# Layer 0 of a two-layer attention network: the evictions, the first head pair's fills and the output projection in another order

## The chip, the cores and the metric

The kernel runs on one core of one Trainium2 chip. A core has a matrix engine (TensorE, PE in the profile, with its weight loads as PEld), three engines for elementwise work (VectorE = DVE, ScalarE = ACT, GpSimd = POOL) and SyncE (SP), which here only issues DMA transfers. Each engine runs its own instructions in the order in which the program has them; semaphores tie the engines together. TensorE writes its results into PSUM, from where VectorE or ScalarE must take them before the space can be used again. ScalarE issues DMA transfers too, in line with its other work.

The metric is the device time of one execution in microseconds (us), and less is better. The kernel before the change took 2998.03 us, the median of three runs (2995.43 to 3001.4).

## What is computed

Eight images of 384 channels and 32 x 32 pixels (1024 tokens) go through two layers. The change is in layer 0, which the reference gives as follows (cut):

```python
def _L0_conv_ref(x, qkv_w, qkv_b, proj_w, proj_b, ...):          # x is the group norm of the image
    tokens = x.reshape(b, c, n).transpose(0, 2, 1)
    qkv = (tokens @ qkv_w + qkv_b).reshape(b, n, 3, NUM_HEADS, HEAD_DIM)   # 8 heads of 48
    q, k, v = ...
    attn = jnp.einsum('bhnd,bhmd->bhnm', q * scale, k)
    attn = jax.nn.softmax(attn + _relative_bias(h, w, ...)[None], axis=-1)
    out = jnp.einsum('bhnm,bhmd->bhnd', attn, v)
    out = out.transpose(0, 2, 1, 3).reshape(b, n, c) @ proj_w + proj_b
    return out.transpose(0, 2, 1).reshape(b, c, h, w)
x = x + _L0_conv_ref(_gn(x), ...)
```

Layer 1 (attention with normalized q and k, and a feed-forward block with quantized activations) follows. The change does not touch it.

## The kernel before

Layer 0 goes image by image (`for b in range(B)`). For each image its q, k and v are computed, then the scores, their exponentials and the weighted values in batches, and last the output projection. The heads are taken as four pairs. A tile of q or k has 128 rows, 64 for each head of a pair: 48 rows (`D0`) are the head's own, and 16 more (`FR`) belong to the fourth pair, whose 48 rows are computed 16 at a time in the spare rows of the three other pairs. So there are six blocks of q and k products, `BLOCKS0` = (pair 0, k), (pair 0, q), (1, k), (1, q), (2, k), (2, q); this text counts them as blocks 0 to 5.

For images 1 to 7 the products run in a form in which each float is cut into a coarse part and a rest. `Ahead.products` (line 664) makes three groups of six matmuls for a block, two into a PSUM tile `pg` and one into a PSUM tile `pm`. `Ahead.take` (line 670) empties them: ScalarE takes `pm` into an SBUF tile `t` (L687), VectorE adds `pg` (L691). `halves` (line 696) then cuts `t` again: ScalarE rounds it into the upper half (L700; `k`, `q` or `th` in the profile) and VectorE subtracts that to have the lower half (L701). Both halves of a block of pair 1 or 2 are stored to HBM (`self.there`, shown as `halves`), the upper half on ScalarE's DMA queue and the lower half on SyncE's (L705: 512 KB each; L707: the 16 spare rows of each head, 64 KB each). Pair 0 is used at once and isn't stored, except for its spare rows.

The scores of a batch use three operand tiles for k and two for q. For k they are the upper half, the lower half, and one mixed tile. In each of them the spare 16 rows, or all 64, must be filled with rows of the other half. For pairs 1 to 3 that happens when they are loaded back (`load_k`, `load_q`). For pair 0 the `move` function (line 714) does it with SBUF to SBUF transfers, `PIECES`: for q six transfers (four of 128 KB into the mixed tile, two of 64 KB into the upper half), for k eight (four of 128 KB into the mixed tile, two of 64 KB into each half). In the profile they are the L716 lines. The pieces for the mixed tile go out in `halves`; the others are handed back and run after the next block's `take`.

Four PSUM tiles of two banks each (`mm2`) are all there is for TensorE's results, taken in turn: two for a block of q and k products, two for a quarter of v (`project_v`, L772, emptied on VectorE at L780 and L784), one for each score product, one for the weighted values and one for each third of the output projection.

The attention of images 1 to 7 is a list of 16 batches per image (`Batches.run`, line 905). A batch makes four score products (L916), VectorE adds the relative bias to each (L923), ScalarE takes exponentials (L927), and TensorE weighs the values (L889) one batch later. Between the score products of a batch and the end of the one before, `between` does other work for units 2n and 2n + 1 of batch n. Unit 3, which is in batch 1, makes the output projection of the image before (`project_out`, L993 and L1009): 36 matmuls over `oT`, with the residual `res` added on VectorE and the result stored by SyncE (L1012).

`oT` holds the weighted values. `divide` normalizes them by a trip through HBM: SyncE stores the sums (L951, L953), GpSimd inverts them (L954), SyncE spreads the inverse (L958, L966), GpSimd multiplies (`multiply`, L970). For the fourth pair SyncE then moves 16 rows each to the places of the three other pairs (L980, six transfers of 64 KB). `later` is a list of work that comes due after so many steps; `take` and `project_v` count as steps.

The crossing from one image to the next (lines 1153 to 1204) emits: blocks 0 and 1 of the next image with their `take`; then block 2, a quarter of v, `halves`, the three other quarters of v; then blocks 3 to 5, each with its `take` and `halves`; then the loads of `res`; then batch 0 of the next image. In `take`, the halves of a block are emitted right behind its eviction, and so stand ahead of the next block's eviction in ScalarE's and VectorE's order. Only block 5's halves are held until `between` of batch 0.

All transfers of ScalarE and SyncE use eight completion semaphores in turn, in the order in which the scheduler has them, and each waits until the transfer that had its semaphore before, eight transfers earlier, has landed. The list of the built program shows these waits for both kernels.

Of the kernel before, what the change touches and what calls it, by code (L numbers as in the profile page):

```python
# [19 lines left out]
F32 = mybir.dt.float32  # L20
F32R = mybir.dt.float32r
AF = mybir.ActivationFunctionType
ALU = mybir.AluOpType
# [16 lines left out]
NP0 = H0 // 2  # L40
NF0 = NP0 - 1
FR = D0 // NF0
# [21 lines left out]
CUT = 4096.0  # L64
# [38 lines left out]
BLOCKS0 = [(0, 1), (0, 0), (1, 1), (1, 0), (2, 1), (2, 0)]  # L103
# [97 lines left out]
class _Weights:  # L201
# [74 lines left out]
def _layer0(tc, ins, x1, sums, shared, weights, beside):  # L276
# [4 lines left out]
    nc = tc.nc  # L281
    x = ins["x"]
# [3 lines left out]
    with ExitStack() as ctx:  # L286
        const = ctx.enter_context(tc.tile_pool(name="a_const", bufs=1))
        qkp = ctx.enter_context(tc.tile_pool(name="a_qk", bufs=2 * NP0 + 1))
# [9 lines left out]
        def flat2(t):  # L298
            return t.rearrange("p h q -> p (h q)")

        later = _Later()
# [4 lines left out]
        SP = S0 - D0  # L306
# [20 lines left out]
        for g in range(P // QT):  # L327
            at = g * QN
            n = min(QN, NREL - at)
# [104 lines left out]
        oT = kept.tile([P, NP0, N], F32, tag="oT", name="oT")  # L434
# [162 lines left out]
        BB = len(BLOCKS0) // 2  # L597
# [35 lines left out]
        class Ahead:  # L633
# [34 lines left out]
                cuts.products(n, i, self.ps[n, i // 2], self.parts[i])  # L668

            def take(self, n):  # L670
                pair, s = BLOCKS0[n]
                name = f"{self.b}_{pair}_{s}"
                here = pair == 0
                t = rest = qkp.tile([P, N], F32, tag="qk", name="t" + name)
                if here and s == 1:
                    self.k[pair] = self.k_tiles(pair)
                elif here:
                    self.q[0] = [
                        qkp.tile([P, N], F32R, tag="qk", name=f"q{i}" + name) for i in range(2)
                    ]  # L680
                    for h in range(NH):
                        self.q[0, h] = [q[:, ts(h, HALF)] for q in self.q[0]]
                else:
                    high = qkp.tile([P, N], F32R, tag="qk", name="th" + name)
                ps = self.ps.pop((n, 0)), self.ps.pop((n, 1))
                by = D0**-0.5 if s == 0 else 1.0
                nc.scalar.activation(  # L687
                    t, flat2(ps[1]), AF.Identity, scale=-by / CUT,
                    bias=bq[:, pair : pair + 1] if s == 0 else bqk[:, s, pair : pair + 1],
                )  # L690
                nc.vector.scalar_tensor_tensor(  # L691
                    t, flat2(ps[0]), by * (1.0 + 1.0 / CUT), t, ALU.mult, ALU.add
                )
                later.step()

                def halves():
                    up, down = (self.q[0] if s == 0 else self.k[0][:2]) if here else (high, rest)
                    if here and s == 0:
                        down = t
                    nc.scalar.copy(up, t)  # L700
                    nc.vector.tensor_sub(down, t, up.bitcast(F32))  # L701
                    for x, (queue, part) in enumerate(((nc.scalar, up), (nc.sync, down))):
                        part = part.bitcast(F32)
                        if not here:
                            queue.dma_start(self.there[s, pair, x], part)  # L705
                        for j in range(2):
                            queue.dma_start(  # L707
                                self.there[s, NF0, x, j * S0 + pair * FR : j * S0 + (pair + 1) * FR],
                                part[j * S0 + D0 : (j + 1) * S0],
                            )  # L710
                    if not here:
                        return []

                    def move(to, row, n, x, at):
                        for j in range(2):
                            (nc.sync if x or row == D0 else nc.scalar).dma_start(  # L716
                                to[j * S0 + row : j * S0 + row + n].bitcast(F32),
                                (up, down)[x][j * S0 + at : j * S0 + at + n].bitcast(F32),
                            )

                    tiles = self.q[0] if s == 0 else self.k[0]
                    for piece in PIECES[s][-1]:
                        move(tiles[-1], *piece)
                    return [
                        lambda to=to, of=of: move(to, *of[1]) for to, of in zip(tiles[:-1], PIECES[s])
                    ]

                return halves

            def k_tiles(self, pair):  # L730
                return [
# [210 lines left out]
        def divide(b, pair):  # L942


            o = oT[:, pair]
            sd = dram.tile([2, N], F32, tag="sd", name=f"sd{b}_{pair}")
            rd = dram.tile([2, N], F32, tag="rd", name=f"rd{b}_{pair}")
            mine = sums[:, b, pair]
            inv = kept.tile([P, 2 * N // P], F32, tag="inv", name=f"inv{b}_{pair}", bufs=2)
            for j in range(2):  # L950
                nc.sync.dma_start(sd[j : j + 1], oT[j * S0 : j * S0 + 1, pair])  # L951
            with nc.allow_non_contiguous_dma(reason="sums"):
                nc.sync.dma_start(mine, sd.rearrange("j (p c) -> (j p) c", c=2 * N // P))  # L953
                nc.gpsimd.tensor_tensor(inv, mine, over.to_broadcast([P, 2 * N // P]), ALU.pow)  # L954

            def keep_inverse():
                with nc.allow_non_contiguous_dma(reason="sums"):
                    nc.sync.dma_start(rd.rearrange("j (p c) -> (j p) c", c=2 * N // P), inv)  # L958

            later.after(2, keep_inverse)  # L960
            rb = []

            def spread():
                rb.append(kept.tile([P, N], F32, tag="rb", name=f"rb{b}_{pair}"))
                for j in range(2):
                    nc.sync.dma_start(rb[0][ts(j, S0)], rd[j].partition_broadcast(S0))  # L966
                later.after(2, multiply)

            def multiply():
                nc.gpsimd.tensor_mul(o, o, rb[0])  # L970
                if b == B - 1:
                    if pair < NF0:
                        for j in range(2):
                            nc.gpsimd.memset(oT[j * S0 : j * S0 + SP, pair], 0.0)
                elif pair == NF0:

                    for c in range(NF0):
                        for j in range(2):
                            row = j * S0 + SP + c * FR
                            nc.sync.dma_start(  # L980
                                oT[j * S0 : j * S0 + SP, c], oT[row : row + FR, pair]
                            )

            later.after(2 if pair == NF0 else 3, spread)

# [52 lines left out]
        parts = [(h, c) for h in range(H0) for c in range(4)]  # L1038
# [16 lines left out]
        for i in range(len(parts) // 2):  # L1055
            later.after(i + (13 if i < 9 else 12), lambda: grow_turns(1))
            at = 1 + i % NF0 if i < 12 else 2 + i % 2
            later.after(i + 10, lambda at=at: grow_loads(1, at))
        qk = project_qk(0, first)
# [17 lines left out]
        for b in range(B):  # L1077

            def beside_unit(i):
                nonlocal xn, ahead, cuts, res  # L1080
                if i == (16 if b == 0 else 1) and b + 1 < B:
                    xn = load(b + 1)
                    for at, stage in zip(
# [1 line left out]
                        group_norm(b + 1, xn),  # L1085
                    ):
                        later.after(at, stage)
                if i == 3 and b > 0:
                    project_out(b - 1, res, range(NF0))
                if b == B - 1:  # L1090
                    for at, work in beside:
# [10 lines left out]
                if b in (1, 2, 3) and i == 12:  # L1102
                    t = shared.weights(f"cw{b}")
# [5 lines left out]
                if b + 1 < B:  # L1109
                    if i == masks[0]:  # L1110
                        ahead = Ahead(b + 1, xn)
# [59 lines left out]
            for k in range(KC):  # L1171
                ahead.mixed(k)

            waits = []

            def take(n):
                nonlocal held_halves
                halves = ahead.take(n)
                if n < BB:
                    cuts.load(n + BB)  # L1180
                if n == BB - 1:
                    ahead.project_v(0)
                while waits:
                    waits.pop(0)()
                if n < len(BLOCKS0) - 1:
                    waits.extend(halves())
                else:
                    held_halves = halves

            for n in range(2):  # L1190
                for i in range(2):
                    ahead.products(cuts, n, i)
            for n in range(2):
                ahead.products(cuts, n, 2)
                take(n)
            for n in range(2, len(BLOCKS0)):
                for i in (2, 0, 1):
                    ahead.products(cuts, n, i)
                take(n)
                if n == BB - 1:  # L1200
                    for m2 in range(1, MT // 2):
                        ahead.project_v(m2)
            place = shared.weights(f"res{b}")
            res = residuals(b, lambda name, place=place: place[:, ts(int(name[-1]), N)])

# [1351 lines left out]
```

## Time and profile before

| | us |
|---|---|
| median of three runs | 2998.03 |
| the profiled execution's own time | 3001.04 |
| its span, first to last instruction | 2999.2 |
| TensorE busy in it | 2900.5 (97%) |
| VectorE busy | 2020.1 (67%) |
| ScalarE busy | 1555.8 (52%) |
| layer 0, eight images with its preparation, ends at about | 1430 |

The page's slices show TensorE at nine tenths or more of nearly every slice in the second half, and at eight tenths in some of the first, where layer 0 runs. These dips come back once for each image. DMA is used most in the same half (150 to 220 GB/s in most slices). A busy share is an average, so it doesn't show where the lost time is; for this one asks for the busy time of stretches of the timeline.

### The profile page before, as it was taken

To read this page: it belongs to the slowest core of one execution; us is meant where nothing else is said; L and a number is where in the kernel's file an instruction comes from. 1 tells how busy PE (TensorE), PEld (TensorE's weight loads), DVE (VectorE), ACT (ScalarE), POOL (GpSimd) and SP (SyncE) were. 2 spreads that over 40 slices of the span, in tenths; PEclk is the share of its full clock that TensorE was granted. 3 is DMA by queue.
4 is the path that set the end of the run, shared out by engine and by line. 5 is a ranking of instruction groups with operands and counts; after the bars stand their busy time and mean duration, and the time that the engine had idled before them with its cause. 6 is when DMAs were issued, how large, how long until landed. Compare 5 with 4: busy or idle time off the path is not lost.

```text
span 2999.2 us, 43573 instructions
## 1 busy us (share of the span) xinstructions
PE 2900.5 (97%) x16850; PEld 1656.4 (55%) x16850; DVE 2020.1 (67%) x2041; ACT 1555.8 (52%) x1888; POOL 492.4 (16%) x318
## 2 busy tenths in 40 slices
PE   8999989899998989989999999999999999999999
PEld 3464554645455464644545656746756746755553
DVE  3976858677675867756474685685785775775746
ACT  2654626454462645445372474574564564564644
POOL 3120202112020211103201301302302302302020
PEclk9999999999999999999999999999999999999999
DMA  7656475655647465473420121211312202112111
GB/s 192 188 170 185 134 216 132 183 158 149 183 119 210 113 181 148 139 206 80 136 76 24 35 78 50 64 53 50 87 31 59 92 21 78 69 39 82 39 45 38
DMA packets 177752, 324.78 MB, mean 108 GB/s; under 512 B 75745, under 2 KB 94673, under 8 KB 176257
## 3 DMA queue, kind: packets, MB, share of 16 engines
q1 hardware_dynamic: 166880, 298.04, 34.5%
q10 hardware_dynamic: 10656, 23.85, 2.9%
q8 instruction: 137, 2.24, 0.3%
q14 instruction: 79, 0.64, 0.1%
HBM read 227.50 MB, written 80.65 MB: 103 GB/s over the span
## 4 chain that ended last, share of the span: by engine, by line
PE 83%; DVE 7%; ACT 4%; DMA 3%; issue 2%; ACTq 1%; SPq 0%; POOL 0%; DVEq 0%
PE o L889 13%; PE s L1909 11%; PE o L1958 11%; PE s L916 9%; PE y2p L2203 6%; PE pg L171 5%; PE y1p L2152 5%; PE pp L993 4%; PE pv L1846 4%; PE pp L2055 3%; PE pm L171 2%; PE s L820 2%; PE pq L1698 1%; DVE t L691 1%; DVE e L923 1%
## 5 line engine op out<-in xcount | busy, mean ns | idle before, releaser
L927 ACT ACTIVATE e<-e 128x1024 f32<-128x1024 f32 x448 | 473.7, 1058 | 271.0 <-DVE e L923 246.2
L923 DVE TENSOR_TENSOR e<-s,grow 128x1024 f32<-128x1024 f32 x448 | 516.9, 1217 | 72.5 <-PE s L916 66.2
L1920 ACT ACTIVATE e<-s,kc 128x512 f32<-128x512 f32 x768 | 464.0, 694 | 172.1 <-PE s L1909 161.3
L889 PE MATMUL o<-e,v 128*64 128x512 f32 x1792 | 416.9, 609 | 24.4 <-DVE e L923 24.4
L1909 PE MATMUL s<-qk,qk 64*64 64x512 f32 x3072 | 418.7, 592 | 1.2 <-DVE oT L1968 1.1
L1958 PE MATMUL o<-e,v 64*64 64x512 f32 x3072 | 414.3, 590 | 0.0
L916 PE MATMUL s<-q,k 64*128 64x512 f32 x2688 | 358.1, 411 | 28.1 <-ACT t L687 24.4
L916 PEld LDWEIGHTS s<-q,k 64*128 64x128 f32 x2688 | 253.5, 192 | 170.3 <-DVE e L923 38.8
L889 PEld LDWEIGHTS o<-e,v 128*64 128x64 f32 x1792 | 123.8, 139 | 262.7 <-issue 242.4
L1935 DVE TENSOR_TENSOR t<-t,e 128x1024 f32<-128x1024 f32 x192 | 231.0, 1221 | 46.0 <-ACT e L1920 45.9
L1909 PEld LDWEIGHTS s<-qk,qk 64*64 64x64 f32 x3072 | 153.9, 132 | 191.2 <-issue 108.9
L1958 PEld LDWEIGHTS o<-e,v 64*64 64x64 f32 x3072 | 159.3, 133 | 169.4 <-issue 142.3
L954 POOL TENSOR_TENSOR inv<-sums,over 128x16 f32<-128x16 f32 x32 | 93.2, 2913 | 845.2 <-DMA sums<-sd 653.4
L2139 DVE TENSOR_REDUCE parts<-y 128x1 f32<-128x1024 f32 x75 | 89.7, 1217 | 103.3 <-ACT y L2136 102.8
L1932 DVE TENSOR_TENSOR t<-e,e 128x1024 f32<-128x1024 f32 x96 | 114.2, 1224 | 59.5 <-ACT e L1920 59.5
L1815 POOL TENSOR_TENSOR hc<-hc,rsqrt 128x32 f32<-128x32 f32 x24 | 141.3, 5888 | 2.0
L1846 PE MATMUL pv<-wv,bx 128*128 128x384 f32 x384 | 128.3, 491 | 0.0
L2055 PE MATMUL pp<-oT,L_attn_proj_wT 128*128 128x512 f32 x288 | 126.3, 595 | 2.1 <-DVE oT L2021 2.1
L993 PE MATMUL pp<-oT,wp 128*128 128x512 f32 x288 | 125.7, 595 | 0.0
L1846 PEld LDWEIGHTS pv<-wv,bx 128*128 128x128 f32 x384 | 119.4, 314 | 9.8 <-ACT e L1920 4.1
L970 POOL TENSOR_TENSOR oT<-oT,rb 128x1024 f32<-128x1024 f32 x32 | 77.5, 2422 | 264.8 <-DMA rb<-rd 131.1
L2152 PE MATMUL y1p<-lun,w 128*128 128x512 f32 x360 | 113.5, 396 | 2.6 <-DVE lun L2102 2.6
(239 smaller groups left out, 4023.9 us busy)
## 6 DMA issues: line engine op xcount, KB each, us to landing
rb<-rd SPq DMA_DIRECT2D x110, 256.0 KB
wc<-cut SPq DMA_DIRECT2D x42, 576.0 KB
k<-halves SPq DMA_DIRECT2D x84, 192.0 KB
wc<-there SPq DMA_DIRECT2D x25, 576.0 KB
halves<-th ACTq DMA_DIRECT2D x28, 512.0 KB
halves<-t SPq DMA_DIRECT2D x28, 512.0 KB
xn<-in_x_dram SPq DMA_DIRECT2D x24, 512.0 KB
res<-in_x_dram SPq DMA_DIRECT2D x24, 512.0 KB
```

The lines of the kernel that those rows point to most:

```text
L889: nc.tensor.matmul(po[ts(j, S0)], v[:, BT * g + i, 2 * pair + j, :], es[i][:, ts(j, HALF)], start=(i == 0), stop=(i == BT - 1),)
L916: nc.tensor.matmul(ss[i][:, j], k[c][ts(j, S0), ts(BT * g + i, P)], q[a][ts(j, S0)], start=(m == 0), stop=(m == 2),)
L923: nc.vector.tensor_add(e.rearrange("p (j q) -> p j q", j=2), ss[i], near(2 * pair, BT * g + i, h, [GW * IW, 2]),)
L927: nc.scalar.activation(e, e, AF.Exp)
L993: nc.tensor.matmul(pps[b, m][:, h], (wp[:, k] if k < NF0 else wl)[:, ts(m, P)], oT[:, k, ts(h, HALF)], start=(k == 0), stop=(k == (NF0 if ...
L1846: nc.tensor.matmul(pv[:, i, 0:C], xt[:, k].rearrange("c (p m) -> c m p", m=MT)[:, 2 * m2 + i], wv[:, k], start=(k == 0), stop=(k == KC - 1),)
L1909: nc.tensor.matmul(s[j][ts(c, QP), i], qk[pair, 1][rows, ts(4 * m2 + 2 * i + c, QP)], qk[pair, 0][rows, ts(h, HALF)], start=True, stop=True,)
L1920: nc.scalar.activation(e[:, ts(i, HALF)], s[j][:, i], AF.Exp, scale=kc[:, pair, j, m : m + 1])
L1935: nc.vector.tensor_add(total[j], total[j], e)
L1958: nc.tensor.matmul(po[ts(j, D1), r], v[keys, 2 * m2 + i, at : at + D1], es[j][keys, ts(i, HALF)], start=(m2 == 0 and i == 0), stop=(m2 == ...
L2055: nc.tensor.matmul(pps[m][:, h], wp[:, k, ts(m, P)], oT[:, k, ts(h, HALF)], start=(k == 0), stop=(k == NP1 - 1),)
L2152: nc.tensor.matmul(py[m][:, h], w1[:, k, ts(m, P)], un[k][i][:, ts(h, HALF)], start=(k == 0 and i == 0), stop=(k == KC - 1 and i == 1),)
```

## The change

`take` is cut in two. It emits ScalarE's eviction at once and gives back two functions: `add` (VectorE's addition) and `halves`. The crossing now orders them:

- blocks 0 and 1 are evicted and added, and only then come both blocks' halves;
- block 2 is evicted and added, then the first quarter of v, its halves and the other quarters;
- block 3 is evicted and added, its halves are held;
- for blocks 4 and 5, ScalarE's eviction comes first, then the former block's halves, then VectorE's addition.

The fills of pair 0 move. q's mixed tile is still filled in `halves`; q's upper half is filled (`fill_q`) behind the second quarter of v; all eight transfers for k (`fill_k`) come between the halves of block 3 and the addition of block 4. All fills are on SyncE's queue; before, two of k's were on ScalarE's. The tile for k's mixed operand is taken only then. The spreading of the fourth pair's rows of `oT` is put off by one step. The output projection moves from unit 3 to unit 1, that is from batch 1 to batch 0 of the next image, where no weighted values are due.

```diff
@@ take
-                nc.vector.scalar_tensor_tensor(
-                    t, flat2(ps[0]), by * (1.0 + 1.0 / CUT), t, ALU.mult, ALU.add
-                )
-                later.step()
+                def add():
+                    nc.vector.scalar_tensor_tensor(
+                        t, flat2(ps[0]), by * (1.0 + 1.0 / CUT), t, ALU.mult, ALU.add
+                    )
+                    later.step()
                 def halves():
...
+                    if pair == 0 and s == 0:
+                        self.q[0] = [up, tile("m")]
...
+                        self.low_q = t
+                        self.move(self.q[0][1], [up, t], PIECES[0][1])
+                return add, halves
+            def fill_q(self):
+                self.move(self.q[0][0], [None, self.low_q], PIECES[0][0][1:])
+            def fill_k(self):
+                parts = self.k[0][:2]
+                self.k[0].append(qkp.tile([P, N], F32R, tag="qk", name=f"km{self.b}"))
+                self.move(self.k[0][2], parts, PIECES[1][2])
+                for to, pieces in zip(parts, PIECES[1]):
+                    self.move(to, parts, pieces[1:])
@@ divide
                 elif pair == NF0:
+                    later.after(1, spread_rows)
@@ beside_unit
-                if i == 3 and b > 0:
+                if i == 1 and b > 0:
                     project_out(b - 1, res, range(NF0))
@@ the crossing
             for n in range(2):
                 ahead.products(cuts, n, 2)
-                take(n)
+                add, halves = ahead.take(n)
+                add()
+                cuts.load(n + BB)
+                splits.append(halves)
+            for halves in splits:
+                halves()
+            held_halves = None
             for n in range(2, len(BLOCKS0)):
                 for i in (2, 0, 1):
                     ahead.products(cuts, n, i)
-                take(n)
+                add, halves = ahead.take(n)
+                if held_halves is not None:
+                    held_halves()
+                if n == 4:
+                    ahead.fill_k()
+                add()
+                held_halves = halves
                 if n == BB - 1:
+                    cuts.load(n + BB)
+                    ahead.project_v(0)
+                    halves()
+                    held_halves = None
                     for m2 in range(1, MT // 2):
                         ahead.project_v(m2)
+                        if m2 == 1:
+                            ahead.fill_q()
```

More of the change, by code (lines that the diff above doesn't have):

```diff
@@ L672, in take @@
                 name = f"{self.b}_{pair}_{s}"
[L673 to L684, printed above, removed]
+                t = qkp.tile([P, N], F32, tag="qk", name="t" + name)
                 ps = self.ps.pop((n, 0)), self.ps.pop((n, 1))
@@ L690, in take, with tile @@
                 )
-                nc.vector.scalar_tensor_tensor(
-                    t, flat2(ps[0]), by * (1.0 + 1.0 / CUT), t, ALU.mult, ALU.add
-                )
-                later.step()
-                def halves():
-                    up, down = (self.q[0] if s == 0 else self.k[0][:2]) if here else (high, rest)
-                    if here and s == 0:
-                        down = t
+                def add():
[3 more added lines that the diff above has]
+                    later.step()
+                def halves():
+                    def tile(name):
+                        return qkp.tile([P, N], F32R, tag="qk", name=name + f"{self.b}_{pair}_{s}")
+                    up, down = tile("h"), t
+                    if pair == 0 and s == 1:
+                        down = tile("l")
+                        self.k[0] = [up, down]
                     nc.scalar.copy(up, t)
                     nc.vector.tensor_sub(down, t, up.bitcast(F32))
-                    for x, (queue, part) in enumerate(((nc.scalar, up), (nc.sync, down))):
+                    for queue, x, part in ((nc.scalar, 0, up), (nc.sync, 1, down)):
                         part = part.bitcast(F32)
-                        if not here:
+                        if pair > 0:
                             queue.dma_start(self.there[s, pair, x], part)
@@ L710, in halves, with move @@
                             )
[L711 to L728, printed above, removed]
+                    if pair == 0 and s == 0:
+                        self.q[0] = [up, tile("m")]
+                        for h in range(NH):
+                            self.q[0, h] = [q[:, ts(h, HALF)] for q in self.q[0]]
+                        self.low_q = t
+                        self.move(self.q[0][1], [up, t], PIECES[0][1])
+                return add, halves
+            def move(self, to, parts, pieces):
+                for row, n, x, at in pieces:
+                    for j in range(2):
+                        nc.sync.dma_start(
+                            to[j * S0 + row : j * S0 + row + n].bitcast(F32),
+                            parts[x][j * S0 + at : j * S0 + at + n].bitcast(F32),
+                        )
+            def fill_q(self):
[6 more added lines that the diff above has]
+                    self.move(to, parts, pieces[1:])
             def k_tiles(self, pair):
@@ L975, in multiply, with spread_rows @@
                 elif pair == NF0:
[L977 to L982, printed above, removed]
+                    later.after(1, spread_rows)
+            def spread_rows():
+                for c in range(NF0):
+                    for j in range(2):
+                        row = j * S0 + SP + c * FR
+                        nc.sync.dma_start(oT[j * S0 : j * S0 + SP, c], oT[row : row + FR, pair])
             later.after(2 if pair == NF0 else 3, spread)
@@ L1172, in _layer0 @@
                 ahead.mixed(k)
[L1174 to L1188, printed above, removed]
             for n in range(2):
@@ L1192, in _layer0 @@
                     ahead.products(cuts, n, i)
+            splits = []
             for n in range(2):
                 ahead.products(cuts, n, 2)
-                take(n)
+                add, halves = ahead.take(n)
[5 more added lines that the diff above has]
+            held_halves = None
             for n in range(2, len(BLOCKS0)):
```

## The prediction, made before the changed kernel was run

> **What bounds the kernel now.** I read the page's busy times, then TensorE's waits, then stretches of the timeline, then single engines over one stretch.
>
> ```profile
> PE 2900.5 (97%) x16850; PEld 1656.4 (55%) x16850; DVE 2020.1 (67%) x2041; ACT 1555.8 (52%) x1888; POOL 492.4 (16%) x318
> ```
>
> TensorE's waits (us in total, times, longest):
>
> ```profile
> PE o L889 <- DVE e L923: 24.4, 9, 3.5
> PE s L916 <- ACT t L687: 24.4, 13, 4.0
> PE vm L772 <- ACT t L687: 11.5, 13, 2.1
> PE vg L772 <- DVE t L691: 6.0, 13, 0.5
> ```
>
> TensorE is the bound, and its four longest waits all lie where one image follows another. Stretches of one such crossing and the steady part behind it (length, busy time by engine, granted clock, DMA):
>
> ```profile
> 366.30:446.00 79.70, 68.83 (x282) 45.90 (x280) 40.84 (x43) 22.00 (x22) 5.29 (x2) 0.96 0.72 212
> 446.00:525.70 79.70, 79.44 (x489) 39.76 (x490) 69.30 (x68) 53.79 (x54) 18.29 (x12) 1.00 0.53 136
> 411.70:415.10 3.40, 0.48 (x4) 0.29 (x4) 1.53 (x2) 1.37 (x2) 0.00 (x0) 1.00 0.69 195
> 415.10:418.50 3.40, 3.40 (x18) 2.26 (x18) 3.40 (x4) 1.24 (x2) 0.00 (x0) 0.50 0.95 312
> 421.90:425.30 3.40, 0.19 (x2) 0.23 (x4) 2.70 (x3) 0.98 (x2) 0.00 (x0) 1.00 0.63 177
> 425.30:428.80 3.50, 3.50 (x10) 1.21 (x9) 3.05 (x3) 3.28 (x4) 0.00 (x0) 0.51 0.83 282
> ```
>
> The steady part has nothing to give. In the crossing TensorE idles 11 us, and behind each long gap it runs one stretch of 3.4 us at half clock. Where the gaps are, TensorE's timeline of that crossing says (start, length, what, idle before and its releaser):
>
> ```profile
> 380.49 0.80 PE L772 MATMUL vm<-wx,xd 128*128 128x384 f32 x3 [1.31 <-ACT t L687]
> 393.27 0.76 PE L772 MATMUL vm<-wx,xd 128*128 128x384 f32 x3 [1.21 <-DVE v L780]
> 409.67 1.03 PE L916 MATMUL s<-q,k 64*128 64x512 f32 x6 [0.38 <-ACT t L687]
> 414.81 5.62 PE L916 MATMUL s<-q,k 64*128 64x512 f32 x30 [2.92 <-ACT t L687]
> 425.11 5.35 PE L889 MATMUL o<-e,v 128*64 128x512 f32 x16 [3.54 <-DVE e L923]
> ```
>
> ScalarE and SyncE around these:
>
> ```profile
> 378.07 1.21 ACTq L716 DMA_DIRECT2D k<-k  x2
> 379.32 1.11 ACT L687 ACTIVATE t<-pm,bq 128x1024 f32<-128x1024 f32 x1 [2.31 <-DMA halves<-k]
> 405.59 1.05 ACT L700 CAST th<-t 128x1024 fp32r<-128x1024 f32 x1 [6.35 <-PE pm L171]
> 413.65 1.11 ACT L687 ACTIVATE t<-pm,bq 128x1024 f32<-128x1024 f32 x1 [1.69 <-issue]
> 400.29 1.14 SPq L716 DMA_DIRECT2D q<-t  x2
> 408.32 2.02 SPq L707 DMA_DIRECT2D halves<-t  x2
> ```
>
> The eviction of block 1 (379.32) stands behind block 0's rounding and four transfers; block 5's (413.65) behind those of block 4.
>
> **The floor.** From the first product of block 0 to the end of the output projection the seven crossings take 78.6, 79.8, 78.3, 79.7, 81.6, 77.1 and 79.3 us, 554.3 in all (starts of matmuls). Undisturbed: six blocks at 3 x 1.40 (397.93 to 399.33 is one group), 25.2; v, 24 groups of 0.52, 12.5; two batches of scores at 2.95 (446 and later), 5.9; one batch of values, 3.6; the projection 15.65 (430.39 to 446.03); 0.35 for the slower first block. Together 63.2, so a crossing loses 16.0.
>
> **The change, part by part.** I follow the second crossing and count from T, the first product of block 3. Waits by name are from the built program's list.
>
> *Eviction of block 1 first.* ScalarE takes block 1 at 374.95 in place of 379.32; VectorE adds by 377.3; v begins at 379.05 without a wait. Block 2's eviction follows both roundings (2 x 1.05) and four issues (2 x 0.8), and ends at 381.1; the second quarter of v needs it at 382.2. Cover 1.1 us; without it TensorE waits that long. The 1.31, the 0.46s and the 0.18 go. The 1.21 at 393.27 came from a subtraction that took 3.42 us beside GpSimd's multiplication; four of seven crossings show such a wait.
>
> ```profile
> 388.12 3.42 DVE L701 TENSOR_TENSOR t<-t,th 128x1024 f32<-128x1024 f32 x1
> 388.06 2.40 POOL L970 TENSOR_TENSOR oT<-oT,rb 128x1024 f32<-128x1024 f32 x1 [11.40 <-DMA rb<-rd]
> ```
>
>  In the new order SyncE has no k transfers ahead of L958, which issues at 376.7 (GpSimd done) in place of 380.5, so the multiplication falls on about 384.6, again beside that subtraction. I keep half of 1.2: 0.6, ends 0 and 1.3.
>
> *Spread of oT, one step later; q's upper fill later.* Before, SyncE had these eight transfers out at T + 5 (401.4 with T at 396.5). Now the fourth of them waits for a weight load issued at about 388.7, which lands 7 us later (as at 384.12), so they are out at about T + 7 (T is 391.7 now); the readers come at T + 12.6 and T + 20. Nothing; without the 3 us to spare the first scores would wait for q's fill too.
>
> *Fills of k later.* This is the costly part. All eight stand on SyncE behind the three stores of block 3's lower half. Block 4's `pm` is done at T + 5.6; eviction to 6.75; then block 3's rounding to R = T + 7.85; the subtraction to 9.1; the stores hold SyncE until about R + 3.75 (408.32 + 2.02, where R was 406.65). Each transfer also waits for the one eight earlier. The four mixed ones issue from R + 3.75 to R + 5.5 (the fourth waits for the 512 KB store, landed R + 5.5). The two for the upper half wait for the last store of block 3 (R + 5.9) and the first mixed fill, and land at R + 8.5 and 9.1 (2.3 us from issue, as q's at 400.29 and 400.84: completion records 402.52 and 403.27). The last fill waits for the 512 KB store of block 4's upper half on ScalarE. Block 5's eviction reuses a tile that block 3's upper stores still read; these land at R + 4.75 (issue 406.68, last completion 411.40). So: eviction R + 4.8 to 5.9, rounding to 7.0, store landed 2.7 later (2.71 at 406.68 and 411.99) at 9.7, last fill issued, landed at R + 12.05 = T + 19.9. The first score product's fourth matmul reads it and would run at T + 12.95. Stall: 6.95 us. Ends: 5.1 if the last fill had only SyncE's issue to wait for (R + 10.2), 9.5 if the store takes its longest in this place (3.77 at 1283.29) and the fill what 64 KB took beside stores (3.8, issue 408.81, landed 412.57).
>
> *ScalarE's eviction ahead of the former halves, blocks 4 and 5; projection behind batch 0.* The 2.92 before the third score product and the 3.54 before the values go: the exponentials of batch 0 (5 us behind the scores) now lie under 15.65 us of projection. Late next would be block 5's addition: rounding of block 4 T + 14.8, subtraction 16.05, addition 17.3; covered by the fill's stall, and worth 3.0 us (2.5 at the fourth score, 0.5 at the first projection tile) if the fills were early. Behind the projection's first third (T + 28) stands its residual: loads issue about T + 20.7, land 4.2 to 5.6 later (as at 415.80), 1 to 3 us in time. In VectorE's order the three residual additions (1.28 each) precede batch 1's additions; the last ends 1.3 us after the projection and TensorE has 2.2 us of scores in free PSUM tiles. Nothing. SyncE's stores of the result now precede q's loads for batch 4 by more, not less.
>
> *Half clock.* One gap in place of two. Of the fourteen gaps of 2.9 us or more, twelve were followed by half clock, 3.41 or 6.83 us of it. Behind the stall I take half a stretch and a whole one, at half speed: (1.7 + 3.4)/2 = 2.6; ends 1.7 and 3.4.
>
> Sum: 63.2 + 0.6 + 6.95 + 2.6 = 73.35 a crossing, 513.5 in seven; gain 40.8. Against the profiled execution's 3001.0 this is 2960; that execution was 3.0 above the median of the runs, so I forecast **2958 us**. Ends: 63.2 + 0 + 5.1 + 1.7 = 70.0 gives 64 us and 2935; 63.2 + 1.3 + 9.5 + 3.4 = 77.4 gives 12.5 us and 2985.
>
> A rule of the Trainium skill would give another clock term. "TensorE: Matmul & The Clock Gate", Part 1, has the clock halve after a window of about 3.4 us that is wholly idle. The trace disagrees: the stretch at 411.7 held 0.48 us of work and half clock followed.
>
> **Rivals.**
> 1. *The few early products keep the clock up.* The stall has three matmuls in it (T + 16.3, 16.9, 17.5). If any work in a stretch were enough, the 2.6 would go: 18 us, 2940. The row at 411.7 speaks against it: 0.04. This is that page's rule carried out.
> 2. *The fills are in time*, if SyncE got to them before block 3's stores. Then block 5's addition sets the start: 63.2 + 0.6 + 3.0 + 1.7 = 68.5, gain 75, 2923. The order on SyncE's queue speaks against it: 0.08.
> 3. *Slower: the chain store, store, fill runs at crowded latency.* Three landings follow each other on one chain (4.75 - 0.9 for block 3's last upper store, 2.7, 2.3). DMA is at 0.95 in such a stretch, and a transfer issued behind a weight load needed 7.1 (384.74 to 391.87). At 7.1 each, 12.4 us are added: 73.35 + 12.4 = 85.8, a loss of 46 us, 3044. It decides from 5.8 us on (79.2 - 73.35). Against it: the weight loads are over by then, and stores in this place took 2.7 in every crossing: 0.10.
> 4. *What is won in front is lost at the fills*, the same chain half as slow: 2992 to 3004: 0.05.
>
> **How the numbers follow.** Forecast 0.73, rivals 0.04, 0.08, 0.10, 0.05. Faster by over 0.2% (6 us, what a measurement can tell): 0.73 + 0.04 + 0.08 = 0.85; within: 0.05; slower: 0.10. The range is the forecast's own ends with rival 1 in it: 2935 to 2985.
>
> **What would show it.** v without waits for L687's successor; the first score product's matmuls waiting for the L719 transfers, some 7 us per crossing, in place of waits for ScalarE; no wait of the values for VectorE; the last k fill issued right when ScalarE's 512 KB store lands; half clock once per crossing. Wrong if scores start within 3 us of block 5's end, or later than 10.

## The result and the profile after

The changed kernel takes 2960.48 us, the median of four runs (2956.39 to 2966.97), beside 2999.24 (2995.43 to 3001.4) for the kernel before: a ratio of 0.9874, with a 95% interval of 0.9853 to 0.9895. Its profiled execution took 2960.66, with a span of 2958.9.

The busy line of the changed kernel's page (busy time, share of the span, instructions):

```profile
PE 2886.9 (98%) x16850; PEld 1657.1 (56%) x16850; DVE 2017.1 (68%) x2041; ACT 1551.8 (52%) x1888; POOL 493.4 (17%) x318
```

TensorE runs as many matmuls as before. Of the 40 us by which the span is shorter, 14 are busy time (2900.5 before; the same matmuls, less of them at half clock), the other 27 idle time. TensorE's list of waits (us in total, times, longest) says which waits these were:

```profile
PE s L920 <- DMA h<-l: 23.7, 7, 4.7
PE s L920 <- issue: 8.5, 2, 4.3
PE s L920 <- DMA l<-h: 6.9, 8, 1.2
PE vm L776 <- DVE v L784: 2.1, 3, 0.9
PE o L893 <- DVE e L927: 0.5, 2, 0.3
```

The three long waits of before (values for VectorE 24.4, scores for ScalarE 24.4, v for ScalarE 11.5) are gone or down to 0.5. In their place the first score product waits for the fills of k (the 8.5 us under `issue` are its first wait in two of the crossings). TensorE's timeline of the second crossing (start, length, what, idle before and its releaser) shows it three times in a row. The second wait is put down to a store of block 4, but it also ends with a fill: the sixth, which landed at 403.32 us.

```profile
401.86 0.76 PE L920 MATMUL s<-h,h 64*128 64x512 f32 x1 [4.70 <-DMA h<-l]
403.46 0.76 PE L920 MATMUL s<-h,h 64*128 64x512 f32 x1 [0.83 <-DMA halves<-h]
405.40 0.79 PE L920 MATMUL s<-h,l 64*128 64x512 f32 x1 [0.87 <-DMA l<-h]
```

The same crossing and a piece of the steady part behind it, as stretches (length, busy time by engine, granted clock, DMA):

```profile
357.99:432.59 74.60, 67.34 (x284) 47.00 (x282) 42.21 (x44) 20.67 (x21) 5.29 (x2) 0.93 0.75 226
432.59:507.19 74.60, 74.60 (x466) 37.73 (x464) 64.47 (x64) 50.25 (x52) 15.35 (x11) 1.00 0.51 130
```

The crossing still idles 7.3 us where it idled 10.9, at a mean clock of 0.93. The seven crossings are measured over the same work as in the prediction: from the first product of block 0 until both batches of scores, batch 0's values and the projection are through. Before, the projection came last; now it comes behind batch 0's scores, and batch 0's values end the stretch. They take 73.1, 74.6, 72.8, 74.6, 72.7, 73.1 and 74.4 us: 515.2 together, 39.1 less than before, nearly all of the 40.3 us by which the span is shorter.

### The profile page after: what moved, and what is told of

Read it like the earlier page. It is cut to its first block, busy times and chain, and to the rows that moved or that the text cites. A ratio compares the mean times of both kernels' runs of the same rounds, so it can differ in the third digit from the quotient of the medians.

```text
span 2958.9 us, 43504 instructions
## 1 busy us (share of the span) xinstructions
PE 2886.9 (98%) x16850; PEld 1657.1 (56%) x16850; DVE 2017.1 (68%) x2041; ACT 1551.8 (52%) x1888; POOL 493.4 (17%) x318
## 4 chain that ended last, share of the span: by engine, by line
PE 85%; DMA 6%; DVE 4%; ACT 2%; issue 2%; SPq 1%; ACTq 0%; POOL 0%; DVEq 0%; POOLq 0%
PE o L893 13%; PE s L1916 11%; PE s L920 11%; PE o L1965 11%; PE y2p L2210 6%; PE y1p L2159 5%; PE pp L997 4%; PE pg L171 4%; PE pv L1853 4%; PE pp L2062 3%; PE pm L171 2%; PE s L824 2%; PE pq L1705 2%; DMA halves<-h 1%; PE o L855 1%
## 5 line engine op out<-in xcount | busy, mean ns | idle before, releaser
L893 PE MATMUL o<-e,v 128*64 128x512 f32 x1792 | 407.7, 598 | 0.5 <-DVE e L927 0.5
L920 PE MATMUL s<-q,k 64*128 64x512 f32 x2016 | 253.8, 397 | 0.0
L920 PEld LDWEIGHTS s<-q,k 64*128 64x128 f32 x2016 | 182.6, 184 | 103.9 <-issue 26.8
```

The source lines that it names most:

```text
L893: nc.tensor.matmul(po[ts(j, S0)], v[:, BT * g + i, 2 * pair + j, :], es[i][:, ts(j, HALF)], start=(i == 0), stop=(i == BT - 1),)
L920: nc.tensor.matmul(ss[i][:, j], k[c][ts(j, S0), ts(BT * g + i, P)], q[a][ts(j, S0)], start=(m == 0), stop=(m == 2),)
```

## The experiments

Eight kernels were run. Beside the first four the kernel before took 3002.8 us, beside the other four 3000.2. The table gives, for each, the median, the ratio to the kernel before with its 95% interval, and from the profiled execution (one for each kernel) the means over the seven crossings: T is the first product of block 3, counted from the first of block 0; "4th" is the start of the fourth score matmul, counted from T; then the crossing's length, and the time at half clock in all seven.

| kernel | median, us | ratio | T | 4th | length | half clock |
|---|---|---|---|---|---|---|
| before | 2999.24 | 1 | 29.82 | 13.54 | 79.18 | 61.4 |
| changed | 2960.48 | 0.9874 [0.9853, 0.9895] | 25.87 | 20.84 | 73.59 | 58.0 |
| projection alone | 2967.52 | 0.9878 [0.9863, 0.9892] | 30.14 | 13.53 | 74.76 | 44.4 |
| projection back | 2989.44 | 0.9950 [0.9937, 0.9962] | 25.97 | 20.86 | 78.24 | 81.9 |
| fills first | 2931.67 | 0.9760 [0.9747, 0.9772] | 26.03 | 13.02 | 69.97 | 37.5 |
| fills and addition first | 2924.44 | 0.9732 [0.9715, 0.9749] | 26.12 | 13.02 | 69.05 | 20.5 |
| mixed tile's fills last | 2958.73 | 0.9856 [0.9837, 0.9874] | 25.88 | 16.00 | 73.15 | 58.0 |
| store on SyncE | 2943.89 | 0.9804 [0.9788, 0.9820] | 25.89 | 18.65 | 71.54 | 47.8 |
| both halves later | 2902.45 | 0.9673 [0.9655, 0.9691] | 26.04 | 13.02 | 65.13 | 0 |
| both, and store on SyncE | 2894.24 | 0.9643 [0.9628, 0.9658] | 25.70 | 13.02 | 63.74 | 0 |

**The output projection by itself, and taken back.** One line of the change put into the kernel before, and the same line undone in the changed one:

```diff
@@ kernel before
-                if i == 3 and b > 0:
+                if i == 1 and b > 0:
                     project_out(b - 1, res, range(NF0))
@@ changed kernel
-                if i == 1 and b > 0:
+                if i == 3 and b > 0:
                     project_out(b - 1, res, range(NF0))
```

> The kernel before with one line of the change: the output projection behind batch 0's scores. Theory (each stall has a price of its own): the wait of the values for VectorE before batch 1's values (3.54 us at 425.11) goes, with the half clock behind it (1.7 us); the stall before the third score product (2.92) stays, since ScalarE still evicts block 5 behind block 4's halves. 4.9 us less in each of seven crossings, about 2965 us. Rival (the gain comes from the evictions put first, and the projection only changes place): the time stays within 10 us of 2999.

> The changed kernel with the projection back behind batch 1's scores. Theory: the stall at the fills of k stays at about 7 to 8 us a crossing, and the values wait for VectorE's exponentials of batch 0 again (3.5 us, with up to a stretch of half clock behind it): 3.5 to 5.2 us more in each of seven crossings, 2985 to 2997 us, the kernel before's time within 0.5%. Rival (with the fills as the one late thing, everything behind them is on time anyway): within 5 us of 2960.

Both theories held: 2967.5 and 2989.4. In the first, the old stall for ScalarE's eviction of block 5 is still there (TensorE's timeline of the second crossing):

```profile
410.19 2.93 PE L916 MATMUL s<-q,k 64*128 64x512 f32 x12 [2.93 <-ACT t L687]
```

In the second, the wait of the values for VectorE is back (TensorE's list of waits):

```profile
PE o L893 <- DVE e L927: 22.5, 8, 3.5
```

By the crossings of one execution each, the projection gives 30.9 us of the 39.1 when it is put in alone and costs 32.5 when it is taken back; the rest gives 6.6 by itself and 8.2 on top of the projection. By medians the projection's part is as plain (0.9878 and 0.9950 on either side of it), but the rest is not: 0.9878 can't be told from the whole change's 0.9874, and the profiled execution of the projection alone was 4.2 us above its median. So how much the rest adds to the projection is open, between nothing and some 8 us. As a balance it is small: up to T it wins 3.85 us a crossing (29.82 against 25.97), and the fills take most of it back.

**The fills first.** The eight fills of k go ahead of block 3's halves in the emitted order, the mixed tile's last; then block 5's addition goes ahead of block 4's halves too.

```diff
@@ fill_k
-                self.k[0].append(qkp.tile([P, N], F32R, tag="qk", name=f"km{self.b}"))
-                self.move(self.k[0][2], parts, PIECES[1][2])
                 for to, pieces in zip(parts, PIECES[1]):
                     self.move(to, parts, pieces[1:])
+                self.k[0].append(qkp.tile([P, N], F32R, tag="qk", name=f"km{self.b}"))
+                self.move(self.k[0][2], parts, PIECES[1][2])
@@ the crossing, fills first
-                if held_halves is not None:
-                    held_halves()
                 if n == 4:
                     ahead.fill_k()
+                if held_halves is not None:
+                    held_halves()
                 add()
@@ the crossing, addition first too
+                if n == 5:
+                    add()
                 if held_halves is not None:
                     held_halves()
-                add()
+                if n < 5:
+                    add()
```

> The changed kernel with the eight fills of k ahead of block 3's stores on SyncE's queue, those for the upper and lower tiles first, the mixed tile's last. Theory (the first scores wait for the last fill, and it is late because of what is ahead of it in the queue and the semaphore it shares with ScalarE's store): the fills land before block 5's products end; what is late then is block 5's addition, a stall of about 3 us in place of 7 to 8, so 4 to 5.3 us less in each of seven crossings, 2923 to 2935 us. Rival (the transfers of this stretch are limited by bandwidth and land when they land, or the stall is ScalarE's, whose rounding of block 3 comes later here): 2955 us or more.

> The kernel with the fills first, and block 5's addition ahead of block 4's halves. Theory: the addition that is late once the fills are early comes 2 us or so earlier (block 4's rounding and subtraction no longer precede it), so the stall before the first scores goes down to 1 us or less and the half clock behind it with it: 2910 to 2925 us, 7 to 20 us below the kernel with the fills first alone. Rival (the addition waits for ScalarE's eviction of block 5, not for the halves): the same as the kernel with the fills first alone, within 4 us.

Both times lie where the theory put them, the second near the upper end and only just apart from the first (the intervals 0.9747 to 0.9772 and 0.9715 to 0.9749 touch). The mechanism held in the main. With the fills first the scores start behind block 5 with no gap (the fourth matmul at T + 13.02, an undisturbed start), and five crossings wait for what was named as late next, block 5's addition, 3.3 us each. But the fills are not all in time. Block 5's products end at T + 12.75; the last fill lands at T + 10.5 to 11.6 in four crossings and only at T + 15.4 to 16.8 in the other three, and the matmuls that read the mixed tile (`km`) wait for it. First the waits of the kernel with the fills first:

```profile
PE s L920 <- DVE t L683: 16.6, 5, 4.5
PE s L920 <- DMA km<-l: 6.4, 5, 2.0
```

Then those of the kernel with the addition first as well:

```profile
PE pp L997 <- DVE e L927: 19.2, 7, 4.1
PE s L920 <- DMA km<-l: 4.2, 4, 1.5
```

The wait for the addition is down to 0.2 us, and half clock from 37.5 us to 20.5. But another wait of nearly the same size stands further on: the output projection waits for a free PSUM tile, which VectorE frees by adding the bias to batch 0's first scores. VectorE's timeline of the second crossing tells why that is late:

```profile
393.91 1.23 DVE L697 TENSOR_TENSOR t<-t,h 128x1024 f32<-128x1024 f32 x1 [2.11 <-ACT h L696]
395.06 3.48 DVE L927 TENSOR_TENSOR e<-s,grow 128x1024 f32<-128x1024 f32 x3
```

Block 4's subtraction stands ahead of the bias additions, and itself waits 2.11 us for ScalarE's rounding. So the stall has moved one step further along VectorE's queue, to work that nobody waits for yet. The kernel with both halves later, below, moves that work.

**What made the fills late.** In the changed kernel SyncE's and ScalarE's queues were read together with the landing of each transfer. In all seven crossings the last fill was issued 0.01 to 0.02 us after ScalarE's 512 KB store of block 4 had landed, as its semaphore demands. Two kernels take that wait away in different manners: one by the order of the fills (mixed tile's last, at the old place), one by giving block 4's upper stores to SyncE, behind the fills.

```diff
@@ mixed tile's fills last: fill_k as above, the crossing unchanged
@@ store on SyncE
-                    for queue, x, part in ((nc.scalar, 0, up), (nc.sync, 1, down)):
+                    for queue, x, part in ((nc.sync if n == 4 else nc.scalar, 0, up), (nc.sync, 1, down)):
```

> The changed kernel with the eight fills of k at the same place behind block 3's stores, but in another order: those for the upper and lower tiles first, the mixed tile's last. Built so, the last fill waits for an earlier fill and no more for ScalarE's 512 KB store of block 4. Theory (the shared semaphore with that store is what makes the last fill late): the fills are all landed at about R + 10 in place of R + 13, the stall before the first scores is 2 to 3 us shorter, 2940 to 2947 us. Rival (the transfers of this stretch land when the bandwidth or SyncE's issue lets them, whatever their order): 2957 to 2964 us.

> The changed kernel with block 4's three upper stores on SyncE's queue, behind the fills of k, in place of ScalarE's. The order of the fills stays. The last fill then shares its semaphore with the third store of block 3's lower half. Theory as before (the wait for ScalarE's store makes the last fill late): 2 to 3 us less in each crossing, 2940 to 2947 us, about as the kernel with the mixed tile's fills last. Rival: 2957 to 2964 us; and if those two kernels come out apart, the order of issue counts by itself.

They came out apart. The store on SyncE gave what the theory said, 2943.9; the other order gave nothing that can be measured against the changed kernel (2958.7), as the rival said. Its fourth score matmul does start early (T + 16.00 in the table), since the upper and lower tiles are filled first, but the fifth reads the mixed tile and waits instead, in all seven crossings:

```profile
PE s L920 <- DMA km<-l: 24.5, 7, 3.9
```

The landing of the last fills in the second crossing shows why they are no earlier (us from issue to landing, from the trace's records; T is 384.42, 384.01 and 382.33 in the three kernels):

```
                             issued   took     ScalarE's 512 KB store issued
changed, 8th fill (64 KB)    403.01   2.35     399.58
other order, 5th (128 KB)    398.53   2.63     399.13
other order, 6th (128 KB)    399.11   4.68
other order, 7th (128 KB)    399.75   4.60
other order, 8th (128 KB)    400.86   3.85
store on SyncE, 8th (64 KB)  398.39   2.44     399.07 (by SyncE)
```

In the other order the last fill no longer waits for the store's landing, and counted from T it is issued 1.7 us earlier (1.66 on the mean of seven crossings); but now it and two before it are on the way together with the store, and take 3.9 to 4.7 us in place of 2.4 (3.1 to 4.7 over all crossings). So it lands at T + 20.70 in place of T + 20.94, 0.2 us earlier (0.4 on the mean). The store delays the fills in two ways, through the semaphore and by what is on the way together; only a fill that is issued ahead of the store is free of both. The runs don't tell how much of the second is the store's own part: its two 64 KB companions are on the way too, and the last fills are here those of 128 KB. The Trainium skill states this second way in "DMA: Bandwidth & Descriptors", section "Issuing engines are not separate DMA queues": transfers run on the same sixteen DMA engines and interleave, whichever engine issued them. The rows above agree.

**Two steps on.** Block 4's halves go behind batch 0's additions and exponentials, together with block 5's; then block 3's upper stores go to SyncE as well, behind the fills.

```diff
@@ both halves later
-                if held_halves is not None:
-                    held_halves()
-                if n < 5:
-                    add()
-                held_halves = halves
+                if n < 5:
+                    if held_halves is not None:
+                        held_halves()
+                    add()
+                    held_halves = halves
+                else:
+                    held_halves = lambda fs=(held_halves, halves): [f() for f in fs]
@@ and store on SyncE
-                    for queue, x, part in ((nc.scalar, 0, up), (nc.sync, 1, down)):
+                    for queue, x, part in ((nc.sync if n == 3 else nc.scalar, 0, up), (nc.sync, 1, down)):
```

> The kernel with the fills first and block 5's addition first, and block 4's rounding, subtraction and stores moved too, behind batch 0's additions and exponentials (with block 5's). What that kernel still waits for is a free PSUM tile before the projection (19.2 us in seven waits for VectorE's addition of batch 0). Theory (that addition is late because block 4's subtraction stands ahead of it on VectorE, waiting for ScalarE's rounding, which waits for stores to land): the addition starts 2 us earlier, the wait goes, 1.3 to 4.1 us less in a crossing and less half clock: 2900 to 2915 us. Rival (the addition waits for the scores, which wait for the mixed tile's fills): within 5 us of 2924.

> The kernel with both halves later, and block 3's upper stores on SyncE's queue, behind the fills, in place of ScalarE's. Theory: ScalarE's eviction of block 5 no longer stands behind the issue of these stores (2.2 us), block 5's addition comes 1 us earlier, where that is what the scores wait for: 0 to 1 us a crossing, 0 to 7 us below the kernel with both halves later. Rival: the stores wait behind the fills, what reads or reuses their tile comes later, and the time is the same or longer.

The first came out at 2902.45, as the theory had it: VectorE's timeline of the second crossing has the bias additions 3.0 us earlier, counted from T (391.76 with T at 377.28, against 395.06 with T at 377.55), and the projection's waits for it are down from 19.2 us to 0.4.

```profile
390.62 1.22 DVE L683 SCALAR_TENSOR_TENSOR t<-pg,t 128x1024 f32<-128x1024 f32 x1 [0.84 <-ACT t L677]
391.76 4.61 DVE L927 TENSOR_TENSOR e<-s,grow 128x1024 f32<-128x1024 f32 x4
```

The second, 2894.24, gave 8.2 us more, a little over the 0 to 7 of its theory, and mostly for a reason that the theory did not have: ScalarE's eviction of block 5 does come 2.2 us earlier (T + 10.0 in place of T + 12.2 in the second crossing), but the fills also run free of ScalarE's stores. In the kernel with both halves later, fills of the mixed tile took up to 5.45 us and TensorE waited 5.8 us for them; here all but one of 28 took 2.3 to 2.6, and the wait is 0.4. This kernel beats both others: 3.6% under the one before. Its second crossing, as a stretch (columns as above):

```profile
349.98:414.27 64.29, 63.45 (x283) 45.01 (x282) 41.88 (x44) 20.82 (x21) 5.29 (x2) 1.00 0.78 228
```

TensorE is busy for 63.45 of 64.29 us, at full clock.

## Why the prediction was right, point by point

The forecast was 2958 us against 2960.48, with the gain where it was put. (Its last step is 0.8 us off: 2998.03 less 40.8 is 2957.2.) Its terms for a crossing, beside what the profiled execution of the changed kernel shows:

| term | predicted | measured | from |
|---|---|---|---|
| floor | 63.2 | 63.05, 63.19 | the two crossings of the last kernel with T undisturbed and no stall at the scores (its mean of seven is 63.74) |
| v | 0.6 | 0.61 | T at 25.87, 25.26 undisturbed |
| stall at the fills | 6.95 | 7.82 | fourth score matmul at T + 20.84, 13.02 undisturbed |
| half clock | 2.6 | 1.96 | 73.59 less 63.2 and the other two |
| crossing | 73.35 | 73.59 | |

*Eviction of block 1 first.* Right: v starts 12.77 us behind block 0's first product in six of seven crossings (12.80 was the plan), and no v product waits for ScalarE. GpSimd's multiplication fell where it was expected (375.92 in the second crossing, 17.9 us behind the first product), beside block 0's or 1's subtraction, which took 3.37 us again. TensorE waited behind it in three of seven crossings (2.1 us in the list of waits), and a fourth began v 0.6 us late; half of 1.2 as a mean was right.

*The fills of k.* The mechanism was right step by step, the size a little low. Block 4's store was issued at T + 14.97 on the mean of seven crossings (T + 14.85 predicted), the last fill right when it landed, and that fill took 2.35 us, as predicted. The step that was mis-sized is "rounding to 7.0, store landed 2.7 later": the store took 3.46 us (3.32 to 3.65), with three or four fills on the way beside it. The 2.7 was taken from stores of the kernel before, which had no fills beside them; and "2.7 in every crossing", as rival 3 puts it, holds for six of seven only (2.71 to 2.93 at block 4's place, 3.77 in the seventh). These 0.76 us and 0.12 of the step before are the 0.87 by which the stall was undersized. The trial with the store on SyncE confirms the term from the other side: it took 2.19 us off the fourth matmul's start, where the prediction's chain gives 1.85 for a last fill that has only SyncE's issue to wait for (R + 10.2 in place of R + 12.05).

*Half clock.* Once per crossing, as said, but longer: 58.0 us of it in seven crossings (6.83 in four of them, 10.24 in three), 8.3 a crossing where the sum had 5.1, and nearly as much as the 61.4 before. The 1.96 in the table is what is left behind the stall; a part of the half clock lies in the wait itself, where it slows the few matmuls between the waits and is counted with the stall. Altogether it cost more than the 2.6: TensorE's busy time is 23.0 us longer than in the last kernel, which runs the same matmuls in these crossings at full clock (2886.9 against 2863.9), 3.3 us a crossing. By the table, the errors in the half clock (0.64) and in the stall (0.87) have opposite signs; the closeness of the sum owes something to that.

*Spread of oT, q's upper fill, the residual, the projection.* Costed at nothing, and nothing shows: no score, no projection tile of layer 0 waits for them. The projection's cover works, since the values wait 0.5 us in all.

*What bounds.* A small misreading without weight: the list of waits has one of 7.4 us at the start of the program (`ph L446`), ahead of the 6.0 that the prediction counts as the fourth. The change doesn't touch it (7.6 after).

*Rivals.* Rival 1 (a few products keep the clock up) fell in all seven crossings. Rival 2 (fills in time) did not happen, but the kernel with the fills first is that case built on purpose: 2923 was worked out for it, 2931.7 came, with the fills late in three crossings and block 5's addition late by 3.3 us in place of 3.0. Rival 3 needed 5.85 us more in a crossing, that is 14.7 us for the chain's three landings in place of the 8.85 of the sum; they took 9.8 (4.02, 3.46 and 2.35). Rival 4 (the gain lost at the fills) is nearly true of the evictions' part by itself: undo the projection, and 13 us remain (2989.4 beside 3002.8). The prediction did not split the gain in this way. It listed eviction and projection together, and the trials show that one line, the projection's, gives most of it: 31 to 32 of the 39 us by the crossings' lengths.

## What to carry to other kernels

Sum the stage as if nothing waited, and compare that floor with the length in the trace: here the floor of 63.2 us against 79.2 said how much was to be had, and four steps later a kernel stood at 63.74. After each step ask which queue holds the late thing up and what stands in it that nobody waits for yet: stores in front of fills, a subtraction whose result is only stored in front of an addition that frees PSUM. Work whose result has no early reader goes last in every in-order queue, and a big store waits until the small transfer that somebody needs has been issued, on whichever queue either of them is.

## What the runs showed of the hardware that was not expected

**The clock falls by a busy share, not by an idle window.** The granted clock changes on a grid of 3.41 us. From 150 to 1290 us of all ten profiles, where the crossings lie, 68 windows at full clock were followed by half clock. In 59 of them TensorE was busy for 1.5 us or less, and only 6 were idle or nearly so (under 0.05 us); no window with so little work kept full clock. Between 1.55 and 1.95 us, 9 windows were followed by half and 13 by full clock. Of the more than 3100 windows with more work than that, none was followed by half. Busy time is that of the profile's records, whose ends are modelled. Two windows of the changed kernel, one behind the other (columns as above; the granted clock is the third number from the end):

```profile
396.69:400.10 3.41, 0.48 (x3) 0.04 (x1) 0.52 (x1) 2.05 (x2) 0.00 (x0) 1.00 0.86 220
400.10:403.52 3.42, 0.82 (x2) 0.38 (x2) 1.84 (x2) 0.00 (x0) 0.00 (x0) 0.50 0.79 250
```

And two of the kernel with fills and addition first, third crossing, where the scores also stood still in between:

```profile
557.03:560.44 3.41, 1.99 (x17) 1.29 (x13) 1.88 (x2) 1.05 (x1) 0.00 (x0) 1.00 0.54 208
560.44:563.85 3.41, 2.78 (x7) 1.38 (x8) 3.41 (x4) 2.75 (x3) 0.00 (x0) 1.00 0.95 268
```

The first was busy for 0.48 us and half clock followed; the third for 1.99, and full clock stayed. So two stalls of 1 to 2 us with work between them cost their own length here, and one that empties more than half of a window costs a stretch of half clock on top. The Trainium skill's "TensorE: Matmul & The Clock Gate", Part 1, names at least one idle window of about 3.4 us as the condition; the length of the window agrees, the condition does not.

**Transfers of one queue pay for stores of another.** A 128 KB fill from SBUF to SBUF took 2.3 to 2.6 us from issue to landing when the next 512 KB store was issued 0.7 us or more behind it (27 of the 28 fills of the mixed tile in the last kernel; one took 3.27), and 3.1 to 4.7 when it was issued from 0.03 us before to 2.2 us behind ScalarE's 512 KB store (the last three fills of the kernel with the mixed tile's fills last, all seven crossings).
